# A graph network's edge loop: which edge rows GpSimd gathers, and where the first of them come from

## The chip, the cores and the metric

The kernel runs on one core of one Trainium2 chip. The metric is the device time of one execution in microseconds (us). The core's engines work side by side, each through its own instructions in order: PE (TensorE), DVE (VectorE), ACT (ScalarE), POOL (GpSimd) and SP (SyncE, which here issues DMAs). ACT and POOL issue DMAs as well. All arithmetic is in float32.

## The reference

One message-passing layer of a graph network with a layer norm ahead of it: 12,500 nodes of 64 features, 412,500 edges of 32 features, sorted by receiver (dst). Cut to what matters:

```python
h = jnp.maximum(_layernorm(x, axis=-1), 0.0)
msg_in = concat([h[src], h[dst], edge_attr_32])           # 64 + 64 + 32
messages = act(msg_in @ W1 + b1) @ W2 + b2                # act is swish
att = softmax(act(msg_in @ Wa1 + ba1) @ Wa2 + ba2, axis=0)  # over all edges
aggregated = segment_sum(messages * att, dst)
out = x + act(concat([h, aggregated]) @ Wu1 + bu1) @ Wu2 + bu2
```

W1 and Wa1 split into three parts, for the sender, the receiver and the edge. The sender's part depends on the node alone, so it can be worked out once per node and looked up per edge.

## The kernel before

**Node stage.** x is read in eight chunks. For each, DVE and ACT normalize the rows (sum, deviation, square, root, reciprocal, cut at zero); PE transposes them into hT (features on the partitions, kept on chip for the whole run); PE multiplies hT with the sender's weights, and SP stores the result as the table ts_d, one row of 128 floats per node (L274). Then PE and DVE make the receiver's table, and ACT's queue stores it as tr_d (L310, L312), and behind it one copy of hT as hT_d (L313), which is read only by the function general, a fallback that doesn't run here. Both tables are double buffered tiles of one pool; the main loop's own tiles take that pool's place, so DVE's first preparations (L421 and on) wait for the last tr_d stores.

**Main loop** (one_pass). The 412,500 edges make 3304 tiles of 125 edges, eight to a group, 413 groups (g). load(g) does what can be done ahead, two groups early (AHEAD = 2):
- POOL issues one indirect DMA per tile (L533), which gathers 125 rows of ts_d, by the sender numbers in src_full, into the group's buffer gs. There are seven such buffers, used in turn; a group's first gather waits until the group seven earlier has let go of the buffer. The tile j = 3 gathers 126 rows (WIDE), one more than it uses.
- SP loads the edges' features (eo, L544) and receiver numbers (dbs, L547) for four groups at a time, and for each group two windows of the receivers' table (wins, L554).
- DVE turns receiver numbers into a selection matrix (L558), and PE multiplies it and the edge features with the windows (L562): what the receivers and edges add, in PSUM (pe).

begin(g): DVE adds the gathered rows (L573) and ACT takes tanh (L576). end(g): DVE forms the messages (L586), and the attention logits (L592, L594, L597); L592 is the last to read gs. Four groups later by_node, out_of, project and put weigh the messages and add them into per-node sums. In the first four groups ACT also fills the two tables for these sums, a quarter each time (L752, twice 1588 columns).

**Chosen groups.** In some groups the last tile isn't gathered. Every third group (EVERY, PHASE: g mod 3 = 1, from 8 to NG - 13) is chosen; POOL then issues seven gathers. For the eighth tile, SP loads the 125 sender numbers (num, L478), DVE works out the sender's column in hT and its half (places, L487 to L493), ACT reads the columns' numbers into registers and copies the 125 columns of hT one by one (columns, L504), DVE clears the wrong half (L567), and PE multiplies them with the sender's weights into the same PSUM tile (L568). The copies are spread over earlier groups: burst(g, 0) after begin and burst(g, 1) after end, by the lists in SLOTS.

The order on DVE, ACT and PE is the program's where an instruction is pinned (pin, keep_in_program_order); what isn't pinned, the DMA issues among it, is placed by a scheduler as early as its inputs allow.

Of the kernel before, what the change touches and what calls it, by code (L numbers as in the profile page):

```python
# [44 lines left out]
F32 = mybir.dt.float32  # L45
I32 = mybir.dt.int32
AF = mybir.ActivationFunctionType
ALU = mybir.AluOpType
# [5 lines left out]
P = 128  # L54
# [18 lines left out]

EVERY = 3
PHASE = 1
SLOTS = (((0, 24), (24, 24)), ((48, 24), (72, 12)), ((84, 24), (108, 17)))
ROUND = 12582912.0
WIDE = 126
EPS = 1e-5
# [11 lines left out]
def gnn_kernel(ctx: ExitStack, tc: tile.TileContext, n_edges, x, src, src_row, dst, dst_row, first, edge,  # L91
# [71 lines left out]


    with tc.tile_pool(name="node1", bufs=1) as node1, \
            tc.tile_pool(name="node", bufs=2) as node, \
# [39 lines left out]

        eps = node1.tile([P, 1], F32, name="eps")
        nc.vector.memset(eps, EPS)
# [103 lines left out]
        pin(nc.scalar.dma_start(tr_d[NP:, :], zero[:WR, :]))  # L312
        pin(nc.scalar.dma_start(hT_d, hT))  # L313

# [79 lines left out]
def one_pass(tc, n_edges, v):  # L394
    nc = tc.nc
    NB, T, NG, NP, NT = (v[k] for k in ("NB", "T", "NG", "NP", "NT"))
    ident, iota_w, bj, dloc, src_full, base_sb, real, unreal, far, wrong = (
        v[k] for k in ("ident", "iota_w", "bj", "dloc", "src_full", "base_sb", "real", "unreal",
                       "far", "wrong"))
# [12 lines left out]
    with ExitStack() as ctx:  # L412
# [43 lines left out]
        with tc.tile_pool(name="work2", bufs=2) as work2, \  # L456
# [14 lines left out]

            chosen = {g for g in range(8, NG - 12) if g % EVERY == PHASE}

            def numbers(g):
                if g in chosen:
                    e = (g * K + K - 1) * EP
                    n = nums[g] = small.tile([P, EP], I32, name="num", bufs=2)
                    nc.sync.dma_start(n, bass.AP(tensor=v["src_row"].tensor,  # L478
                                                 offset=v["src_row"][:, e:].offset, ap=[[0, P], [1, EP]]))

            def places(g):
                if g not in chosen:
                    return
                n = nums[g]
                near = small.tile([1, EP], F32, name="near", bufs=1)
                to = small.tile([1, EP], I32, name="to", bufs=2)
                pin(nc.vector.tensor_scalar(to, n[0:1], 1, None, op0=ALU.logical_shift_right))  # L487
                m = NB // 2
                pin(nc.vector.tensor_scalar(near, to, 1.0 / m, 0.5 / m - 0.5, op0=ALU.mult, op1=ALU.add))
                pin(nc.vector.tensor_scalar(near, near, ROUND, None, op0=ALU.add))  # L490
                pin(nc.vector.tensor_scalar(near, near, ROUND, float(1 - m * P), op0=ALU.subtract, op1=ALU.mult))
                pin(nc.vector.scalar_tensor_tensor(to, to, float(P), near, op0=ALU.mult, op1=ALU.add))
                pin(nc.vector.tensor_scalar(n, n, 1, None, op0=ALU.bitwise_and))  # L493
                cols[g] = small.tile([P, EP], F32, name="cols", bufs=2), to

# [10 lines left out]
            def burst(g, k):  # L506
                for i in range(EVERY):
                    columns(g + 3 + i, *SLOTS[EVERY - 1 - i][k])

# [6 lines left out]
            def registers(g, engine, at, base=base_sb, top=NP - 1):  # L516
# [4 lines left out]
                for i in range(n):  # L521
                    at[g + i] = regs[i]

            def load(g):

                t = g * K
                if g % NQ == 0:
                    registers(g, ENG.SP, at_sp)
                full = gather.tile([P, K, C], F32, name="gs")
                gs = gss[g] = full[:EP]  # L530
                for j in range(K - (g in chosen)):
                    rows = WIDE if j == 3 else EP
                    nc.gpsimd.indirect_dma_start(  # L533
                        out=full[:rows, j, :], out_offset=None, in_=ts_d[:, :],
                        in_offset=bass.IndirectOffsetOnAxis(ap=src_full[:rows, t + j:t + j + 1], axis=0))
                if g % NQ == 0:
# [24 lines left out]
                for q in range(H):  # L561
                    pin(nc.tensor.matmul(pe[:, 2 * q:2 * q + 2, :], eo[:, q * EP:(q + 1) * EP],  # L562
                                         win[:, q // 2, :, :], start=True,
                                         stop=q < H - 1 or g not in chosen))
                if g in chosen:
# [4 lines left out]
            def begin(g):  # L570

                n = K - (g in chosen)
                pin(nc.vector.tensor_tensor(gss[g][:, :n, :], pes[g][:, :n, :], gss[g][:, :n, :], ALU.add))  # L573
                if n < K:
                    pin(nc.vector.tensor_copy(gss[g][:, n, :], pes[g][:, n, :]))
                pin(nc.scalar.activation(pes[g], gss[g], AF.Tanh))  # L576
# [161 lines left out]
            for g in range(NG):  # L738
# [39 lines left out]
                for t in {NG - 5: [0, 1], NG - 4: [2, 3], NG - 2: range(4, NT)}.get(g, []):  # L778
                    inputs(t)
                if g == min(30, NG):  # L780
                    pin(nc.vector.tensor_reduce(far[:, 0:1], dloc, AX.X, ALU.max))
                    pin(nc.vector.tensor_scalar(far[:, 0:1], far[:, 0:1], -float(R - 1), None,
                                                op0=ALU.add))
# [357 lines left out]
```

## Time and profile before

| | |
|---|---|
| median of 3 runs (lowest, highest) | 4832.74 us (4832.67, 4833.29) |
| the profiled execution, its own time | 4832.74 us |
| its span in the profile | 4831.0 us |
| busy: POOL, DVE, PE, ACT | 78%, 71%, 50%, 46% |
| gathers on POOL | 3173, mean 1183 ns |
| mean DMA rate | 82 GB/s |

Busy shares are means over the span. In a row of a group of instructions the columns are: line, engine, operation, tiles written and read, shape, count, then busy us and mean ns of one, then the engine's idle time just before these instructions and what ended most of it. "issue" is time in which the engine waited for nothing that the profile shows. In a timeline the columns are start, duration, engine, line, operation, tiles, count and the idle time before in brackets. POOL's time for a gather is the time of issuing it, not that of moving the rows.

### The profile page before, as it was taken

The page shows a single profiled execution, that of the slowest core. Times are in us where ns is not written, and L with a number is a line of the kernel's source. Part 1 is how long each engine was busy: PE and PEld are TensorE (multiplying, and loading weights), DVE is VectorE, ACT ScalarE, POOL GpSimd, SP SyncE. Part 2 cuts the span into 40 slices and gives each one's busy share as a digit, 9 for nine tenths or more (in the row PEclk, how much of TensorE's full clock was granted, in tenths as well). Part 3 has the DMA queues.
Part 4 walks back from the last instruction along what each step waited for, and adds up shares of the span by engine and source line. Part 5 has one row for each costly group of instructions (what it writes and reads, how often), then busy time and mean ns, then how long its engine had stood idle before and what let it go on. Part 6 is the DMA issues. An engine that isn't in the chain of part 4 may idle for free. (4 is left out here: it accounts for less than half of the span.)

```text
span 4831.0 us, 81829 instructions
## 1 busy us (share of the span) xinstructions
PE 2424.5 (50%) x11509; PEld 1945.6 (40%) x11509; DVE 3435.4 (71%) x9793; ACT 2202.4 (46%) x17625; POOL 3770.8 (78%) x3198
## 2 busy tenths in 40 slices
PE   5455555555555444444544554544444444445455
PEld 4344444344444433333433443433333334434344
DVE  6677777777777676766766776776776767767677
ACT  3444444444444444444444444444444444444412
POOL 4777777777777777777777777777777777777775
PEclk8555566666555556665566555566666566555666
DMA  7333333333333333333333333333333333333333
GB/s 253 77 78 85 88 77 85 90 76 84 85 75 78 73 75 78 71 76 78 72 76 77 70 78 78 69 78 78 70 78 73 75 78 71 76 77 72 76 93 82
DMA packets 364009, 395.99 MB, mean 82 GB/s; under 512 B 213813, under 2 KB 293236, under 8 KB 363074
## 3 DMA queue, kind: packets, MB, share of 16 engines
q0 software_dynamic: 240624, 206.55, 19.3%
q1 hardware_dynamic: 121458, 174.49, 15.3%
q10 hardware_dynamic: 1376, 9.67, 0.5%
q14 instruction: 457, 3.74, 0.3%
q8 instruction: 94, 1.54, 0.1%
HBM read 361.63 MB, written 25.72 MB: 80 GB/s over the span
## 5 line engine op out<-in xcount | busy, mean ns | idle before, releaser
L533 POOL DMA_INDIRECT gs<-ts_d,src_sb x3173 | 3753.7, 1183 | 1018.5 <-issue 957.7
L562 PE MATMUL pe<-wins,eo 128*125 128x256 f32 x3304 | 1523.6, 637 | 1522.4 <-DVE eo L558 1256.3
L504 ACT COPY cols<-hT 128x1 f32 x16375 | 1619.4, 187 | 739.3 <-issue 735.7
L562 PEld LDWEIGHTS pe<-wins,eo 128*125 128x125 f32 x3304 | 997.8, 319 | 1843.4 <-DVE eo L558 1342.9
L573 DVE TENSOR_TENSOR gs<-pe,gs 125x1024 f32<-125x1024 f32 (+1 forms) x413 | 487.3, 1180 | 1067.3 <-DMA gs<-ts_d,src_sb 1053.4
L576 ACT ACTIVATE pe<-gs 125x1024 f32<-125x1024 f32 x413 | 424.3, 1027 | 1695.8 <-DVE gs L573 831.0
L640 DVE TENSOR_SCALAR wt<-iota_w,dloc,p 125x40 f32<-125x40 f32 x3304 | 766.3, 352 | 1.8
L646 PE MATMUL sp<-wt,acts 125*65 125x40 f32 x6608 | 648.6, 269 | 13.1 <-DVE wt L640 11.6
L646 PEld LDWEIGHTS sp<-wt,acts 125*65 125x65 f32 x6608 | 608.4, 185 | 23.8 <-DVE wt L640 19.6
L657 PEld LDWEIGHTS mt<-ss,w2u 65*128 65x128 f32 x826 | 209.4, 281 | 349.2 <-issue 206.1
L616 PE MATMUL mt<-ident,mx 125*128 125x125 f32 x110 | 48.1, 438 | 589.5 <-DVE sums L675 563.1
L558 DVE TENSOR_SCALAR eo<-dbs,bj 64x250 f32<-64x250 int32 x826 | 301.0, 395 | 17.7 <-DMA dbs<-in_dst_row_dram 8.3
L657 PE MATMUL mt<-ss,w2u 65*128 65x40 f32 x826 | 187.8, 321 | 250.5 <-DVE gm L623 213.2
L594 DVE TENSOR_TENSOR pe<-pe,w_all 125x512 f32<-125x512 f32 x413 | 288.7, 699 | 13.7
L592 DVE SCALAR_TENSOR_TENSOR pe<-pe,gs 125x512 f32<-125x512 f32 x413 | 287.1, 695 | 10.8
L586 DVE SCALAR_TENSOR_TENSOR acts<-pe,gs 125x512 f32<-125x512 f32 x413 | 283.8, 687 | 12.1 <-ACT pe L576 2.6
L597 DVE TENSOR_REDUCE lg<-pe 125x8 f32<-125x512 f32 x413 | 284.1, 688 | 10.8
L616 PEld LDWEIGHTS mt<-ident,mx 125*128 125x128 f32 x110 | 20.0, 182 | 600.6 <-issue 597.5
L678 DVE COPY stand<-nmax 64x40 f32 x826 | 211.5, 256 | 3.3
L675 DVE TENSOR_TENSOR sums<-sums,mt 64x40 f32 x606 | 114.1, 188 | 4.9 <-PE mt L657 0.8
L671 DVE SCALAR_TENSOR_TENSOR sums<-sums,scale,mt 64x40 f32 x220 | 55.7, 253 | 84.6 <-PE mt L657 82.5
L357 DVE TENSOR_SCALAR bu<-mt,w_all 64x256 f32<-64x256 f32 (+1 forms) x50 | 23.9, 477 | 92.0 <-PE mt L348 91.6
(124 smaller groups left out, 1106.8 us busy)
## 6 DMA issues: line engine op xcount, KB each, us to landing
eo<-in_edge_dram SPq DMA_DIRECT2D x103, 500.0 KB
dbs<-in_dst_row_dram SPq DMA_DIRECT2D x206, 250.0 KB
gs<-ts_d,src_sb POOLq DMA_INDIRECT x3173
wins<-tr_d SPq DMA_DIRECT2D x826, 32.0 KB
num<-in_src_row_dram SPq DMA_DIRECT2D x131, 62.5 KB
ts_d<-ts SPq DMA_DIRECT2D x5, 896.0 KB
tr_d<-tr ACTq DMA_DIRECT2D x5, 896.0 KB
hT_d<-hT ACTq DMA_DIRECT2D x1, 3136.0 KB
```

The lines of the kernel that those rows point to most:

```text
L504: pin(nc.scalar.copy(to[:, first + i:first + i + 1], hT[:, bass.ds(regs[i], 1)]))
L533: nc.gpsimd.indirect_dma_start(out=full[:rows, j, :], out_offset=None, in_=ts_d[:, :], in_offset=bass.IndirectOffsetOnAxis(ap=src_full[:ro ...
L558: pin(nc.vector.tensor_scalar(eo[:WR, e], db[:, e], bj[g // NQ % 2 * WR:(g // NQ % 2 + 1) * WR, g, h:h + 1], None, op0=ALU.is_equal))
L562: pin(nc.tensor.matmul(pe[:, 2 * q:2 * q + 2, :], eo[:, q * EP:(q + 1) * EP], win[:, q // 2, :, :], start=True, stop=q < H - 1 or g not in ...
L573: pin(nc.vector.tensor_tensor(gss[g][:, :n, :], pes[g][:, :n, :], gss[g][:, :n, :], ALU.add))
L576: pin(nc.scalar.activation(pes[g], gss[g], AF.Tanh))
L592: pin(nc.vector.scalar_tensor_tensor(att, th[:, :, 0:U], 1.0, gs[:, :, 0:U], op0=ALU.add, op1=ALU.mult))
L594: pin(nc.vector.tensor_tensor(att, att, wa2[:EP, None, :].to_broadcast([EP, K, U]), ALU.mult))
L597: pin(nc.vector.tensor_reduce(lgs[s][:, k:k + K], att, AX.X, ALU.add))
L640: pin(nc.vector.tensor_scalar(wt[:, j, :], iota_w[:EP, j // H, :], dloc[:, g * K + j:g * K + j + 1], p[:, k + j:k + j + 1], op0=ALU.is_equ ...
L646: pin(nc.tensor.matmul(sp, acts[g % ACTS][:, j, :], wt[:, j, :], start=j == 0, stop=j == K - 1))
L657: pin(nc.tensor.matmul(pp, w2u.rearrange("s h u -> s (h u)"), sps.pop(g), start=True, stop=True))
```

## The change

There are two groups of edits.

- The 126-row gather is dropped: all gathers have 125 rows. The chosen groups are two of every five (g mod 5 = 1 or 4) in place of one of three; their 125 columns are copied in five lots of 24, 24, 24, 24 and 29, two lots in each group, in the five bursts from five groups ahead on. The small tiles num, to and cols have three buffers instead of two.
- Groups 0 to 3 do not use ts_d. Right at the start ACT's queue loads the sender numbers of their 32 tiles, and POOL gathers rows of the input x itself (64 floats). In load(g) the new function features normalizes these rows on the edges, PE transposes them, and PE multiplies them with the sender's weights into pe; begin(g) copies pe instead of adding. The store of hT_d leaves ACT's queue and is written in the loop, in seven pieces at g = 20 to 26, on SP.

```diff
@@ -71,11 +71,11 @@
-EVERY = 3
-PHASE = 1
-SLOTS = (((0, 24), (24, 24)), ((48, 24), (72, 12)), ((84, 24), (108, 17)))
+LOTS = ((0, 24), (24, 24), (48, 24), (72, 24), (96, EP - 96))
+ROUNDS = 5
+SLOTS = {1: ((5, 1), (4, 0), (4, 1), (3, 0), (3, 1)), 4: ((5, 0), (5, 1), (4, 0), (4, 1), (3, 0))}
 ROUND = 12582912.0
-WIDE = 126
+RAW = 4
 EPS = 1e-5
@@ -161,6 +161,15 @@
+
+    raw_src = const.tile([P, RAW * K], I32, name="raw_src")
+    nc.scalar.dma_start(raw_src, src[:, :RAW * K])
+    raws = [gather.tile([P, K, C], F32, name="gs") for _ in range(RAW)]
+    for g in range(RAW):
+        for j in range(K):
+            nc.gpsimd.indirect_dma_start(
+                out=raws[g].rearrange("p k c -> p (k c)")[:EP, j * D:(j + 1) * D], out_offset=None, in_=x[:, :],
+                in_offset=bass.IndirectOffsetOnAxis(ap=raw_src[:EP, g * K + j:g * K + j + 1], axis=0))
@@ -204,7 +213,7 @@
-        eps = node1.tile([P, 1], F32, name="eps")
+        eps = const.tile([P, 1], F32, name="eps")
@@ -310,7 +319,6 @@
         pin(nc.scalar.dma_start(tr_d[NP:, :], zero[:WR, :]))
-        pin(nc.scalar.dma_start(hT_d, hT))
@@ -469,12 +477,12 @@
-            chosen = {g for g in range(8, NG - 12) if g % EVERY == PHASE}
+            chosen = {g for g in range(8, NG - 12) if g % ROUNDS in SLOTS}
                     e = (g * K + K - 1) * EP
-                    n = nums[g] = small.tile([P, EP], I32, name="num", bufs=2)
+                    n = nums[g] = small.tile([P, EP], I32, name="num", bufs=3)
                     nc.sync.dma_start(n, bass.AP(tensor=v["src_row"].tensor,
@@ -483,7 +491,7 @@
                 near = small.tile([1, EP], F32, name="near", bufs=1)
-                to = small.tile([1, EP], I32, name="to", bufs=2)
+                to = small.tile([1, EP], I32, name="to", bufs=3)
                 pin(nc.vector.tensor_scalar(to, n[0:1], 1, None, op0=ALU.logical_shift_right))
@@ -491,7 +499,7 @@
                 pin(nc.vector.tensor_scalar(n, n, 1, None, op0=ALU.bitwise_and))
-                cols[g] = small.tile([P, EP], F32, name="cols", bufs=2), to
+                cols[g] = small.tile([P, EP], F32, name="cols", bufs=3), to
@@ -504,8 +512,10 @@
             def burst(g, k):
-                for i in range(EVERY):
-                    columns(g + 3 + i, *SLOTS[EVERY - 1 - i][k])
+                for i in (3, 4, 5):
+                    slots = SLOTS.get((g + i) % ROUNDS, ())
+                    if (i, k) in slots:
+                        columns(g + i, *LOTS[slots.index((i, k))])
@@ -521,18 +531,43 @@
+            def features(g):
+
+                gs = gss[g] = v["raws"][g][:EP]
+                xg, xm = (gs[:, h * H:(h + 1) * H, :].rearrange("p k (r d) -> p (k r) d", d=D) for h in range(2))
+                total = small.tile([EP, K], F32, name="raw_t", bufs=1)
+                pin(nc.vector.tensor_reduce(total, xg, AX.X, ALU.add))
+                pin(nc.vector.scalar_tensor_tensor(xm, total[:, :, None].to_broadcast([EP, K, D]), -1.0 / D, xg,
+                                                   op0=ALU.mult, op1=ALU.add))
+                pin(nc.scalar.activation(xg, xm, AF.Square))
+                rstd = small.tile([EP, K], F32, name="raw_r", bufs=1)
+                pin(nc.vector.tensor_reduce(rstd, xg, AX.X, ALU.add))
+                pin(nc.scalar.activation(rstd, rstd, AF.Sqrt, bias=v["eps"][:EP], scale=1.0 / D))
+                pin(nc.vector.reciprocal(rstd, rstd))
+                pin(nc.vector.scalar_tensor_tensor(xg, xm, 0.0, rstd[:, :, None].to_broadcast([EP, K, D]),
+                                                   op0=ALU.max, op1=ALU.mult))
+                pt = one_ps.tile([P, 4, P], F32, name="mt")[:, :, :EP]
+                for q in range(H):
+                    pin(nc.tensor.transpose(pt[:, q, :], xg[:, 2 * q:2 * q + 2, :], ident[:EP, :EP]))
+                to = raw_to[g] = v["raws"][g][:, H:, :EP]
+                pin(nc.scalar.copy(to, pt))
+
+            raw_to = {}
+
             def load(g):
                     registers(g, ENG.SP, at_sp)
-                full = gather.tile([P, K, C], F32, name="gs")
-                gs = gss[g] = full[:EP]
-                for j in range(K - (g in chosen)):
-                    rows = WIDE if j == 3 else EP
+                if g < RAW:
+                    features(g)
+                else:
+                    gss[g] = gather.tile([P, K, C], F32, name="gs")[:EP]
+                gs = gss[g]
+                for j in range(0 if g < RAW else K - (g in chosen)):
                     nc.gpsimd.indirect_dma_start(
-                        out=full[:rows, j, :], out_offset=None, in_=ts_d[:, :],
-                        in_offset=bass.IndirectOffsetOnAxis(ap=src_full[:rows, t + j:t + j + 1], axis=0))
+                        out=gs[:, j, :], out_offset=None, in_=ts_d[:, :],
+                        in_offset=bass.IndirectOffsetOnAxis(ap=src_sb[:, t + j:t + j + 1], axis=0))
                 if g % NQ == 0:
@@ -561,7 +596,10 @@
                                          win[:, q // 2, :, :], start=True,
-                                         stop=q < H - 1 or g not in chosen))
+                                         stop=g >= RAW and (q < H - 1 or g not in chosen)))
+                    if g < RAW:
+                        pin(nc.tensor.matmul(pe[:, 2 * q:2 * q + 2, :], raw_to[g][:, q, :], v["w_pair"][:, 0],
+                                             start=False, stop=True))
                 if g in chosen:
@@ -570,7 +608,10 @@
                 n = K - (g in chosen)
-                pin(nc.vector.tensor_tensor(gss[g][:, :n, :], pes[g][:, :n, :], gss[g][:, :n, :], ALU.add))
+                if g < RAW:
+                    pin(nc.vector.tensor_copy(gss[g], pes[g]))
+                else:
+                    pin(nc.vector.tensor_tensor(gss[g][:, :n, :], pes[g][:, :n, :], gss[g][:, :n, :], ALU.add))
                 if n < K:
@@ -777,6 +818,10 @@
                     inputs(t)
+                if 20 <= g < 27:
+                    n = -(-(NB // 2) // 7)
+                    q = slice((g - 20) * n, min((g - 19) * n, NB // 2))
+                    nc.sync.dma_start(v["hT_d"][:, q, :], v["hT"][:, q, :])
                 if g == min(30, NG):
```

The short hunk that passes src_sb in place of src_full to one_pass is left out.

More of the change, by code (lines that the diff above doesn't have):

```diff
@@ L396, in one_pass @@
     NB, T, NG, NP, NT = (v[k] for k in ("NB", "T", "NG", "NP", "NT"))
-    ident, iota_w, bj, dloc, src_full, base_sb, real, unreal, far, wrong = (
-        v[k] for k in ("ident", "iota_w", "bj", "dloc", "src_full", "base_sb", "real", "unreal",
+    ident, iota_w, bj, dloc, src_sb, base_sb, real, unreal, far, wrong = (
+        v[k] for k in ("ident", "iota_w", "bj", "dloc", "src_sb", "base_sb", "real", "unreal",
                        "far", "wrong"))
```

## The prediction

> **What bounds the kernel now.** I read the page first, then the instructions of the gather line, POOL's timeline, and the start of the run in ten-microsecond windows and as a timeline.
>
> ```profile
> span 4831.0 us, 81829 instructions
> ...
> L533 POOL DMA_INDIRECT gs<-ts_d,src_sb x3173 | 3753.7, 1183 | 1018.5 <-issue 957.7
> ...
> L504 ACT COPY cols<-hT 128x1 f32 x16375 | 1619.4, 187 | 739.3 <-issue 735.7
> ...
> L573 DVE TENSOR_TENSOR gs<-pe,gs 125x1024 f32<-125x1024 f32 (+1 forms) x413 | 487.3, 1180 | 1067.3 <-DMA gs<-ts_d,src_sb 1053.4
> ```
>
> POOL does almost nothing but issue gathers. DVE, the busiest of the others, waits for gathered rows (1053 of 1067 us). POOL's own idle time is "issue": no engine holds it. The next two answers are the gather line's first and last start, and POOL's timeline (start, duration, idle before).
>
> ```profile
> L533 POOL DMA_INDIRECT gs<-ts_d,src_sb x3173: 992/1209/1646, 51.0 to 4773.4; - x199
> ```
>
> ```profile
> 1008.37 1.22 POOL L533 DMA_INDIRECT gs<-ts_d,src_sb  x1 [0.30 <-issue]
> 1009.89 0.99 POOL L533 DMA_INDIRECT gs<-ts_d,src_sb  x1 [0.30 <-issue]
> 1011.19 1.21 POOL L533 DMA_INDIRECT gs<-ts_d,src_sb  x1 [0.30 <-issue]
> 1012.70 1.21 POOL L533 DMA_INDIRECT gs<-ts_d,src_sb  x1 [0.30 <-issue]
> ```
>
> One gather in each group is short: 1.30 us from start to start where the others take 1.51. It is the one of 126 rows (j = 3); groups with seven gathers keep it at that place. From 51.0 to 4773.4 there are 3172 intervals: 413 of 1.30 us, 2759 long ones, and 3.0 us of extra waits between 85 and 93 us (rows with 1.66, 1.71 and 0.50 us idle, released by earlier gathers' DMAs). So a long interval is (4722.4 - 3.0 - 413 x 1.30) / 2759 = 1.516 us with its small disturbances. After the last gather's start 57.6 us remain.
>
> The start, by windows (columns: window, length, busy PE, PEld, DVE, ACT, POOL, clock, DMA share, GB/s), then by timeline:
>
> ```profile
> 50.00:60.00 10.00, 9.91 (x46) 8.41 (x46) 6.39 (x12) 0.00 (x0) 7.19 (x6) 1.00 0.74 272
> 60.00:70.00 10.00, 8.63 (x39) 6.76 (x37) 6.32 (x11) 0.00 (x0) 8.13 (x7) 1.00 0.82 291
> 70.00:80.00 10.00, 0.16 (x1) 0.00 (x0) 3.76 (x23) 0.00 (x0) 7.86 (x8) 0.72 0.93 348
> ```
>
> ```profile
> 74.17 0.89 ACTq L313 DMA_DIRECT2D hT_d<-hT  x1
> ...
> 77.11 0.40 DVE L421 MEMSET bases<- 1x414 int32 x1 [4.00 <-DMA tr_d<-tr]
> ...
> 83.71 0.22 DVE L470 COPY w2u<-mt 65x64 f32<-65x64 f32 x1
> 92.20 1.12 DVE L558 TENSOR_SCALAR eo<-dbs,bj 64x250 f32<-64x250 int32 x4 [8.27 <-DMA dbs<-in_dst_row_dram]
> ...
> 97.83 1.23 DVE L573 TENSOR_TENSOR gs<-pe,gs 125x1024 f32<-125x1024 f32 x1 [4.51 <-PE pe L562]
> ...
> 102.21 0.70 DVE L592 SCALAR_TENSOR_TENSOR pe<-pe,gs 125x512 f32<-125x512 f32 x1
> ```
>
> The main loop's compute cannot begin before the tr_d stores have landed (77.1); DVE then prepares its tiles until 83.9 and waits for dbs, which lands behind the hT_d store. Group 0's buffer is last read by L592, until 102.9. That costs nothing now: seven buffers hold 56 gathers, so POOL needs it back only at about 137.
>
> **Count and pace of the gathers.** Chosen groups rise from 131 to 157 (g mod 5 = 1: 78, = 4: 79, between 8 and 400), so the main stream loses 26 gathers, and 32 more leave it for the early ones: 3173 - 58 = 3115. All now have 125 rows. The first saves 58 x 1.516 = 87.9 us, the second costs 413 x (1.516 - 1.30) = 89.2 us. The two cancel: 3115 x 1.516 = 4722 us, against 4722 + 1 now. So the time hangs on when the main stream runs without a stop.
>
> **The early gathers.** Their row indices are 16 KB; the first x chunk (256 KB) is issued at 0.92 and used at 3.74, so I put their arrival at 3.7. No row shows a gather of 256-byte rows; I take the 125-row interval: 3.7 + 32 x 1.514 = 52 us, as ts_d is ready (51.0). Bounds: 1.30 us each (done at 45, then waiting for ts_d) and 2.4 (done at 80). Either is free as long as POOL must stop later anyway, which is the next point. The Trainium skill (DMA: Bandwidth & Descriptors, Specifications) puts the least transfer for line rate at 512 B; half rows speak against this edit, but no run here shows it and it moves none of the terms.
>
> **The new wait.** The early gathers fill four of the seven buffers. Groups 4, 5 and 6 take the other three: 52 + 24 x 1.514 = 88.5. Group 7 then needs group 0's buffer, and POOL is in order: every later gather queues behind that one. Its release, in the new order on DVE, from 83.9 with durations of the same shapes (reduction or combination of 125x512: 0.69; a square of 512: 0.63; a square root of 8: 0.30; reciprocal 0.19; four transposes 1.12; copy 0.59; L558 twice 0.8; eight matmuls 3.75):
> - features(0): reduce, centre, square, reduce, root, reciprocal, scale = 4.2, to 88.1; transposes and copy to 89.9; L558 beside them, to 89.0.
> - features(1) to 93.1 on DVE; PE's group 0 matmuls to 94.2; group 0's copy (1.2, from L573) to 95.4.
> - ACT: copy of features(1) to 95.9, table load 1.28, tanh 1.03 to 98.2, then the two table fills of L752 (1.51 each) to 101.2. All stand in order ahead of features(2)'s square, 101.8.
> - features(2), which load(2) puts ahead of end(0): reduce 102.6, second table load to 103.1, root, reciprocal, scale to 104.4; L558 to 105.2; L586 and L592 to 106.7.
>
> So POOL's group 7 starts at 106.7 where it could have at 88.5. Group 8 needs end(1), by the same steps at 118.6; POOL gets there 12.1 us after group 7, at 118.8: no second stop. From group 2 on no features stand in the way.
>
> The ACT table load of before takes 1.28 us and tanh follows at once (99.12, then 100.42), after idle time. The Trainium skill (ScalarE: Activation LUTs, What ACT_TABLE_LOAD costs) adds a drain of 1.38 us to every switch; by that, two exposed switches would make the release 2.8 us later and the total 2.8 us more. I go by the row.
>
> **What moves that chain.** The seven pieces of the hT_d store are not pinned. In the built order they stand on SP right behind the last ts_d store and ahead of the first edge load, not at groups 20 to 26; so they are issued from about 48 us, beside the tr_d stores on ACT's queue (49 to 74). They no longer stand in front of dbs, which is then there before DVE asks. But tr_d ends the wait at 77.1. The store's 3136 KB at the 432 GB/s of the window 10 to 20 us is 7.4 us of all DMA engines; the windows above leave free 2.6 + 1.8 + 0.5 = 4.9 us. Bounds for the delay of tr_d: nothing (it fits the gaps), 2.5 (gaps full) and 7.4 (tr_d stands behind all of it). I take 4.5, between the last two, because DVE already waits for these stores five times (1.74, 1.15, 2.37, 0.71, 2.19 us). The early gathers meet the x loads while the DMA share is 0.79 to 1.04; DVE waits 0.44 us for the third chunk: I add 0.7 (0 to 2).
>
> Release: 106.7 + 4.5 + 0.7 = 112.
>
> **What I cost at nothing.** 26 more chosen groups: on ACT 26 x (1619 + 739) / 131 = 468 us, or 1.1 us a group on top of (2202 + 736) / 413 = 7.1, of 11.5; on DVE six place operations, one mask and one copy, 2.1 us each time, 0.13 us a group on 8.3. POOL's pace covers both; without that cover they would be 468 and 55 us. On SP, 26 more num loads (about 0.4 us of issue each) and the seven hT_d issues (under 0.9 us each, in the stretch from 47.7 to 77 where SP issues nothing). The end of the run (57.6 us) has no chosen group and stays.
>
> **Sum.** From group 7's first gather 3115 - 24 = 3091 are left, 3090 intervals: last start 112 + 3090 x 1.516 = 4796.4, now 4773.4: +23 us. Span 4854; the profiled execution took 4832.74, its span plus 1.7, which is also the median of the three runs: **4855.7 us**. In general the change is the release minus 89.0 us.
>
> **Rivals.**
> 1. Not slower: group 0's buffer comes free early, because the features run ahead of the tr_d stores' end or tanh isn't held. It decides below 98.7 us (+9.7 us, 0.2%, about what a measurement can tell from no change); floor 88.5. Time 4832 to 4842. For: dbs is early now. Against: DVE's order has the features behind the tiles of 83.9, and fourteen steps follow. 0.08.
> 2. The hT_d store fits the gaps: release 107.4, 4851 us. For: the DMA share there is 0.74 to 0.82. 0.25.
> 3. Compute no longer keeps up in groups with 53 columns: 1% over POOL's pace in all groups would be 47 us: 4903. Against: 8.3 of 11.5 us on the fullest engine. 0.05.
> 4. The fourth gather is short for its place, not its rows. Then 413 x 0.216 = 89 us come back: 4767. Against: nothing else sets it apart. 0.03.
> 5. The start is worse still (release beyond 120, as when early gathers hold the x loads): above 4864. 0.04.
> The forecast itself has 0.55.
>
> **Range.** Release 102 (no delay, and steps 5 us shorter than their rows) to 120 gives +13 to +31; the pace is uncertain by 0.001 us x 3090 = 3 us: 4843 to 4867. Slower by over 0.2%: 0.55 + 0.25 + 0.05 + 0.04 = 0.89; within: 0.08; faster: 0.03.
>
> **What would show it.** No gather of 1.00 us in the main stream and a steady 1.51; 32 gathers from about 4 to 52 us; an idle stretch of POOL of some 20 us before the 25th main gather, released by DVE near 112; hT_d issued about 48 us; tr_d's last wait later than 77.1. If POOL runs on through 90 us, or waits for buffers in mid-run, I am wrong.

## The result, and the profile after

The changed kernel takes **4863.53 us** (median of four runs, 4860.96 to 4864.56), the kernel before 4832.97 beside it (four runs, 4832.67 to 4833.29): ratio 1.0062, 95% interval [1.0045, 1.008]. It is slower by more than 0.2%, as forecast; the time lies inside the range and 7.8 us above the number. The profiled execution took 4863.94 us, its span 4862.2 against 4831.0: +31.2 where +23 was forecast.

The page of the changed kernel first (gathers are now L568, column copies L512, the addition of gathered rows L614):

```profile
span 4862.2 us, 88819 instructions
...
L568 POOL DMA_INDIRECT gs<-ts_d,src_sb x3115 | 3775.1, 1212 | 972.1 <-issue 893.4
...
L512 ACT COPY cols<-hT 128x1 f32 x19625 | 1925.2, 187 | 959.4 <-issue 936.9
...
L614 DVE TENSOR_TENSOR gs<-pe,gs 125x1024 f32<-125x1024 f32 (+1 forms) x409 | 478.9, 1171 | 1012.5 <-DMA gs<-ts_d,src_sb 1001.0
```

Fewer gathers with a longer mean take about as long as before (3775 us, 3754 before), and DVE still waits 1001 us for gathered rows. So POOL is still the bound, and 26 more chosen groups cost ACT and DVE nothing that counts. POOL's idle time is no longer all "issue"; its waits, by releaser (sum in us, times, longest in us):

```profile
POOL gs L568 <- issue: 893.4, 2930, 0.3
POOL gs L568 <- DVE pe L635: 23.8, 5, 22.6
```

One wait of 22.6 us is the new thing. POOL's timeline shows its place, and what comes ahead of it and after:

```profile
45.15 4.91 POOL L170 DMA_INDIRECT gs<-in_x_dram,raw_src  x1 [0.30 <-issue]
...
58.04 1.21 POOL L170 DMA_INDIRECT gs<-in_x_dram,raw_src  x1 [0.30 <-issue]
59.55 1.21 POOL L568 DMA_INDIRECT gs<-ts_d,src_sb  x1 [0.30 <-issue]
...
94.53 1.28 POOL L568 DMA_INDIRECT gs<-ts_d,src_sb  x1 [0.30 <-issue]
118.42 1.21 POOL L568 DMA_INDIRECT gs<-ts_d,src_sb  x1 [22.61 <-DVE pe L635]
...
129.01 1.21 POOL L568 DMA_INDIRECT gs<-ts_d,src_sb  x1 [0.30 <-DVE pe L633]
```

The early gathers end at 59.2 instead of 52. Groups 4 to 6 follow at once; then POOL stands still until 118.42, where 112 was forecast. Group 8 (129.01) waits no second time. The gather line's answer (min/median/max ns, first and last start) has no 126-row gather left and gives the pace:

```profile
L568 POOL DMA_INDIRECT gs<-ts_d,src_sb x3115: 1205/1209/1684, 59.5 to 4805.2; - x195
```

From 118.42 to 4805.2 there are 3090 intervals of 1.5168 us (forecast 1.516); 57.0 us follow the last start (57.6). Last, the timeline of the start, all engines, for the chain that ends in the release (by the program, L633 is the last to read group 0's buffer; it ends at 117.47, 0.95 us ahead of POOL's gather, and the view names L635, the next instruction of DVE, which ran meanwhile):

```profile
45.06 3.59 DVE L203 TENSOR_TENSOR dloc<-dst_sb,base_p 125x3304 f32<-125x3304 int32 x1
51.63 2.47 DVE L317 TENSOR_TENSOR tr<-pn,w_all 128x512 f32<-128x512 f32 x4
52.21 8.13 SPq L824 DMA_DIRECT2D hT_d<-hT  x7
...
88.38 0.40 DVE L429 MEMSET bases<- 1x414 int32 x1 [4.44 <-issue]
94.99 0.69 DVE L539 TENSOR_REDUCE raw_t<-gs 125x8 f32<-125x512 f32 x1
106.27 1.22 DVE L612 COPY gs<-pe 125x1024 f32<-125x1024 f32 x1 [2.17 <-PE pe L601]
109.60 1.51 ACT L793 ACTIVATE sums<-start 128x1588 f32<-128x1588 f32 x1
111.02 1.51 ACT L793 ACTIVATE stand<-start 128x1588 f32<-128x1588 f32 x1
113.06 1.28 ACT L545 ACT_TABLE_LOAD   x1
114.36 0.30 ACT L545 ACTIVATE raw_r<-raw_r,eps 125x8 f32<-125x8 f32 x1
116.77 0.70 DVE L633 SCALAR_TENSOR_TENSOR pe<-pe,gs 125x512 f32<-125x512 f32 x1
```

The receivers' numbers (L203) start at 45.06; the same instruction of before starts at 40.95. The first tr operation comes at 51.63 (before 47.64). From there to the first preparation after the tr_d stores (88.38), which I call the tr stretch, it is 36.75 us, before 29.47 (47.64 to 77.11). All seven pieces of the hT_d store are issued at 52 to 60 us, between these two, and none at groups 20 to 26. From the first reduction of the features (94.99) to the end of L633 (117.47) the chain takes 22.5 us, as it was worked out.

### The profile page after: what moved, and what is told of

The parts are those of the page before. It is cut to its first block, busy times and chain, and to the rows that moved or that the text cites. A ratio compares the mean times of both kernels' runs of the same rounds, so it can differ in the third digit from the quotient of the medians.

```text
span 4862.2 us, 88819 instructions
## 1 busy us (share of the span) xinstructions
PE 2447.0 (50%) x11609; PEld 1966.1 (40%) x11609; DVE 3519.7 (72%) x10021; ACT 2514.4 (52%) x20891; POOL 3838.3 (79%) x3172
## 5 line engine op out<-in xcount | busy, mean ns | idle before, releaser
L568 POOL DMA_INDIRECT gs<-ts_d,src_sb x3115 | 3775.1, 1212 | 972.1 <-issue 893.4
L512 ACT COPY cols<-hT 128x1 f32 x19625 | 1925.2, 187 | 959.4 <-issue 936.9
L614 DVE TENSOR_TENSOR gs<-pe,gs 125x1024 f32<-125x1024 f32 (+1 forms) x409 | 478.9, 1171 | 1012.5 <-DMA gs<-ts_d,src_sb 1001.0
L681 DVE TENSOR_SCALAR wt<-iota_w,dloc,p 125x40 f32<-125x40 f32 x3304 | 779.2, 368 | 1.2
L687 PE MATMUL sp<-wt,acts 125*65 125x40 f32 x6608 | 653.2, 270 | 12.3 <-DVE wt L681 10.3
L635 DVE TENSOR_TENSOR pe<-pe,w_all 125x512 f32<-125x512 f32 x413 | 288.7, 699 | 13.8
L633 DVE SCALAR_TENSOR_TENSOR pe<-pe,gs 125x512 f32<-125x512 f32 x413 | 287.2, 695 | 10.7
L627 DVE SCALAR_TENSOR_TENSOR acts<-pe,gs 125x512 f32<-125x512 f32 x413 | 283.8, 687 | 10.7 <-ACT pe L617 1.4
L606 PEld LDWEIGHTS pe<-stack,cols 128*125 128x125 f32 x314 | 92.7, 295 | 25.6
```

The source lines that it names most:

```text
L512: pin(nc.scalar.copy(to[:, first + i:first + i + 1], hT[:, bass.ds(regs[i], 1)]))
L568: nc.gpsimd.indirect_dma_start(out=gs[:, j, :], out_offset=None, in_=ts_d[:, :], in_offset=bass.IndirectOffsetOnAxis(ap=src_sb[:, t + j:t ...
L633: pin(nc.vector.scalar_tensor_tensor(att, th[:, :, 0:U], 1.0, gs[:, :, 0:U], op0=ALU.add, op1=ALU.mult))
L635: pin(nc.vector.tensor_tensor(att, att, wa2[:EP, None, :].to_broadcast([EP, K, U]), ALU.mult))
L681: pin(nc.vector.tensor_scalar(wt[:, j, :], iota_w[:EP, j // H, :], dloc[:, g * K + j:g * K + j + 1], p[:, k + j:k + j + 1], op0=ALU.is_equ ...
L687: pin(nc.tensor.matmul(sp, acts[g % ACTS][:, j, :], wt[:, j, :], start=j == 0, stop=j == K - 1))
```

## The experiments

Twelve kernels ran in three sets, each set on another chip, and a ratio is always against the kernel before on the same chip. On the first chip it took 4833.93 us, within 1 us of the time beside the result, so there I also compare with the 4863.53 us of the changed kernel. On the second it took 4860.54 (4841.69 to 4865.88, 17 runs), on the third 5230.97 (5175 to 5240); there I compare parts of the traces, and say so. Edits are shown against the changed kernel, and for the three named "before" against that one. No kernel leaves work out; rows beyond 125 land in partitions that nobody reads.

**The short gather alone.** Is the fourth gather short for its 126 rows, and does the change's loss of these rows carry its price?

```
-        gss[g] = gather.tile([P, K, C], F32, name="gs")[:EP]
+        full = gather.tile([P, K, C], F32, name="gs")
+        gss[g] = full[:EP]
...
+        rows = 126 if j == 3 else EP
-            out=gs[:, j, :], out_offset=None, in_=ts_d[:, :],
-            in_offset=bass.IndirectOffsetOnAxis(ap=src_sb[:, t + j:t + j + 1], axis=0))
+            out=full[:rows, j, :], out_offset=None, in_=ts_d[:, :],
+            in_offset=bass.IndirectOffsetOnAxis(ap=v["src_full"][:rows, t + j:t + j + 1], axis=0))
```

> The changed kernel with one thing put back: the tile j = 3 of groups 4 to 412 gathers 126 rows again. My theory (a gather's time on POOL goes by its rows: 1.30 us from start to start with 126, 1.516 with 125, and POOL sets the pace): 409 gathers x 0.216 us = 88 us less than the changed kernel's 4863.5, so 4775 us; the stop of POOL ahead of group 7 stays, about 1 us longer since POOL gets there earlier. Rival (the fourth gather was short for its place, or compute with two chosen groups of five can't follow a faster POOL): 4863, or between 4775 and 4863 with DVE no longer waiting for gathers.

Measured: 4775.63 us (4775.15 to 4776.72), ratio 0.988 [0.9865, 0.9895]. Its page:

```profile
span 4773.4 us, 88819 instructions
L570 POOL DMA_INDIRECT gs<-ts_d,src_sb x3115 | 3685.5, 1183 | 972.9 <-issue 896.6
```

The mean gather is 1183 ns again, as in the kernel before, and 88 us are gone with the wait at the start still there (23.59 us). So the change with the 126th row put back is faster than both kernels. Rival 4 falls: with 125 rows in the fourth place the gather was long, with 126 it is short.

**The early gathers alone.** Without them (RAW = 0, and no raw gathers ahead of the node stage) POOL should meet no wait, and the node stage should be on time again.

```
-RAW = 4
+RAW = 0
...
-    raws = [gather.tile([P, K, C], F32, name="gs") for _ in range(RAW)]
+    raws = []
```

> The changed kernel without the early gathers: groups 0 to 3 gather ts_d rows like the rest, features and the extra matmuls are gone; chosen groups and 125 rows as in the changed kernel, hT_d pieces still right behind ts_d. My theory: the node stage goes back to its old times (first gather at 51 to 52 us, first tr_d piece on DVE at 47.6 instead of 51.6), POOL makes no stop, and 3146 intervals x 1.516 us = 4769 follow: last start 4821, span 4878, time about 4880. So the early gathers would be worth 16 us in the changed kernel, not the 48.5 us that 32 intervals are. Rival (the early gathers only cost: they delay the node stage and make POOL stop, and give nothing): at or below 4863. Rival on the node stage (it is late for the hT_d store and not for the early gathers): first gather near 55 us here too.

Measured: 4880.72 us (4879.86 to 4882.81), ratio 1.0098 [1.0083, 1.0114]. The first gather starts at 49.94 and no stop follows. The receivers' numbers start at 41.15 and the first tr operation at 47.72, the times of before: the lateness of the node stage (4.0 us) belongs to the early gathers. The tr stretch is 34.9 us (to 82.58), still above the 29.5 of before: most of the 7.3 us is not theirs. And the early gathers gain: 32 x 1.516 = 48.5 us taken from the main stream, less 9.6 (first main gather 59.55, not 49.94), less 22.4 (the stop), leaves 16.5 us; the two times differ by 17.2.

**The hT_d store really late.** Pinned, its pieces stay at groups 20 to 26.

```
-                    nc.sync.dma_start(v["hT_d"][:, q, :], v["hT"][:, q, :])
+                    pin(nc.sync.dma_start(v["hT_d"][:, q, :], v["hT"][:, q, :]))
```

> The changed kernel with the hT_d store's seven pieces pinned on SP, so that they stand at groups 20 to 26. My theory (beside the tr_d stores they take DMA time from them): the stretch from the first tr_d piece on DVE to the first preparation (36.8 us in the changed kernel, 29.5 in the kernel before) goes back to about 30, group 0's buffer comes free about 7 us earlier (111 instead of 118.4), and the time falls by as much, to 4856.5; the pieces at groups 20 to 26 cost nothing, since POOL doesn't wait there. Rival (the tr_d stores are slow for the early gathers' backlog, or the store fits the gaps): the stretch stays near 36 us and the time at 4863.

Measured: 4854.07 us, ratio 1.0041 [1.0028, 1.0055]: 9.5 us less than the changed kernel. The tr stretch is 28.1 us (51.14 to 79.23), and POOL goes on at 108.86 instead of 118.42, 9.56 earlier:

```profile
108.86 1.21 POOL L568 DMA_INDIRECT gs<-ts_d,src_sb  x1 [13.11 <-DVE pe L635]
```

So the store issued at 52 us costs 8.6 us of the tr stretch, and about 9.5 of the time, all through the release. The pieces, now issued between 249 and 313 us, show no cost there: the time falls by as much as the release moves. The 4.5 us that the forecast gave this store were too little. Not all of it is waiting for stores: late in the stretch DVE waits for PE, whose granted clock there is low (two rows of the changed kernel):

```profile
75.32 1.29 DVE L317 TENSOR_TENSOR tr<-pn,w_all 128x512 f32<-128x512 f32 x2 [2.33 <-PE pn L315]
70.00:80.00 10.00, 8.48 (x25) 6.96 (x26) 5.69 (x10) 0.00 (x0) 8.04 (x7) 0.66 0.86 293
```

From 70 to 80 us the clock (third figure from the right) is 0.66. With the store pinned, PE has done most of these products by 70 us, at a clock of 1.00 in the window from 60 to 70.

**One buffer more.** An eighth gather buffer (and seven of another pool's eight, for the room) moves the wait from group 7 to group 8.

```
-    gather = ctx.enter_context(tc.tile_pool(name="gather", bufs=7))
+    gather = ctx.enter_context(tc.tile_pool(name="gather", bufs=8))
...
-    ACTS, WINS, AHEAD = 8, 3, 2
+    ACTS, WINS, AHEAD = 7, 3, 2
```

> The changed kernel with eight gather buffers instead of seven (and seven acts buffers instead of eight, to make room). My theory (POOL stops because groups 4 to 6 use up the buffers before group 0's comes free at 118.4): POOL now goes on through group 7, stops eight gathers later, at about 108 instead of 95.9, and goes on at 118.4 as before, one group further: 8 x 1.516 = 12.1 us less, 4851.4 us. Rival (the stop costs nothing, because compute is behind anyway and would make POOL wait later): 4863.

Measured: 4851.27 us, ratio 1.0036 [1.0022, 1.005], 12.3 us less than the changed kernel. POOL's timeline:

```profile
106.95 1.21 POOL L568 DMA_INDIRECT gs<-ts_d,src_sb  x1 [0.30 <-issue]
118.43 1.21 POOL L568 DMA_INDIRECT gs<-ts_d,src_sb  x1 [10.27 <-DVE pe L635]
```

The release is where it was, 118.4. POOL only gets to the wait later, one group of eight gathers (12.1 us) further on. This is the mechanism of the forecast, a buffer held by the chain, seen from the other side.

**The rows in the kernel before.** All gathers with 125 rows:

```
-                    rows = WIDE if j == 3 else EP
+                    rows = EP
```

> The kernel before with one edit: the tile j = 3 gathers 125 rows like the others. My theory (the pace on POOL goes by rows, nothing else is near its limit): 413 x (1.516 - 1.301) = 89 us more than 4833, so 4922 us, with all gathers near 1.209 us. Rival (the fourth place is what makes it short, or the 126th row is only a side effect of something else in the change): 4833.

Measured on the second chip: 4930.8 us, ratio 1.0158 [1.0131, 1.0186]. By the medians it is 70 us more than the kernel before on that chip, whose runs spread over 24 us; 89 were expected. In the trace the first and last gather start 4819.9 us apart, 4722.3 in the trace of before from the first chip: 97.6, of which 413 x 0.216 = 89 are the rows, and most of the rest a slightly longer interval on that chip. The dropped row has a price in either kernel; its size in the kernel before is less certain than the 88 us of the first experiment.

**Rows by place**, one run: 125, 126, 127 and 128 rows, by j mod 4.

```
-                    rows = WIDE if j == 3 else EP
+                    rows = EP + j % 4
```

> The kernel before with 125, 126, 127 and 128 rows in turn over the tiles j = 0 to 3 and again 4 to 7; the extra rows land in partitions that nothing reads. It is to show what sets a gather's issue time. If it goes by how evenly the rows divide over the DMA engines (the Trainium skill, DMA: Bandwidth & Descriptors, Why a DMA increments its semaphore by 16 and not by 1: the largest number up to 16 that divides the row count, so 5, 14, 1 and 16), then 125: 1.21 us, 126: 1.00, 127 longest, 128 shortest or like 126. If only odd against even counts: 127 like 125, 128 like 126. If any count above 125 is short: all three others near 1.00. Time by the second: 3173 gathers, half at 1.516 and half at 1.30 from start to start: about 4833 - 0.215 x (1540 - 413) = 4590 us; in the first case anywhere, for the 127 rows.

POOL's timeline, the first four gathers of one group:

```profile
1001.59 1.21 POOL L533 DMA_INDIRECT gs<-ts_d,src_sb  x1 [0.30 <-issue]
1003.11 0.99 POOL L533 DMA_INDIRECT gs<-ts_d,src_sb  x1 [0.30 <-issue]
1004.41 2.56 POOL L533 DMA_INDIRECT gs<-ts_d,src_sb  x1 [0.30 <-issue]
1007.27 0.96 POOL L533 DMA_INDIRECT gs<-ts_d,src_sb  x1 [0.30 <-issue]
```

In this order they have 125, 126, 127 and 128 rows: 1.21, 0.99, 2.56 and 0.96 us. 127 rows take over twice as long as 126, so it is not the amount. Count and place go together in this run, but the place alone is ruled out by the runs around it: with 125 rows everywhere no place is short, and with 126 everywhere (next) all are near 1.00. The run took 5698.28 us.

**All gathers with 126 rows.** If POOL's issue were the only bound, this would be some 600 us faster.

```
-                    rows = WIDE if j == 3 else EP
+                    rows = WIDE
```

> The kernel before with 126 rows in every tile; the 126th row is read by nothing. My theory (POOL's pace is the only limit): 2759 x 0.215 = 593 us less, 4240 us, at 1.30 us a gather and 10.0 us a group, which compute (DVE 8.3 us a group) still follows. Rival (another limit comes up between 11.4 and 10.0 us a group: the time a gather's rows need to land, or DVE with its waits): the time ends between 4240 and 4833, POOL's idle time grows, and DVE's waits for gathers (1067 us before) go to nothing if it is DVE.

A miss on the whole line: 5921.24 us, ratio 1.2198 [1.2165, 1.2232]. The gathers did become short, but POOL waits for buffers (its semaphore wait ahead of a group's gathers has a median of 7.4 us, 0.04 in the kernel before), and ACT is slow by itself. The groups of that kernel's trace:

```profile
L533 POOL DMA_INDIRECT gs<-ts_d,src_sb x3173 | 3174.0, 1000 | 2644.2 <-issue 2505.8 <-DMA ts_d<-ts 48.4 <-ACT cols L504 20.4
L504 ACT COPY cols<-hT 128x1 f32 x16375 | 1906.7, 188 | 3016.2 <-issue 3001.6 <-PE pe L562 4.0 <-DVE pe L592 3.0
L573 DVE TENSOR_TENSOR gs<-pe,gs 125x1024 f32<-125x1024 f32 (+1 forms) x413 | 486.2, 1177 | 61.3 <-issue 29.6 <-remote 20.0 <-DMA gs<-ts_d,src_sb 1.6
```

DVE no longer waits for gathers (1.6 us). The column copies, which run one after another in the kernel before, come singly here, with 0.5 to 1.2 us of idle time ahead of each that the trace puts down to no other engine ("issue", 3001.6 us in all, 735.7 before; 757.1 on this same chip with 125 rows everywhere). ACT's timeline:

```profile
2000.73 0.19 ACT L504 COPY cols<-hT 128x1 f32 x1 [0.54 <-issue]
2001.44 0.19 ACT L504 COPY cols<-hT 128x1 f32 x1 [0.52 <-issue]
2002.18 0.19 ACT L504 COPY cols<-hT 128x1 f32 x1 [0.55 <-issue]
2003.56 0.19 ACT L504 COPY cols<-hT 128x1 f32 x1 [1.19 <-issue]
```

The trace does show where the delay sits. Ahead of each copy ACT works out its address in registers (FUSED_REGOPS; min/median/max ns); here are the kernel before on the first chip, this kernel, and the changed kernel as it ran on the third chip (below):

```profile
L504 ACTq FUSED_REGOPS  x16375: 37/37/43, 126.2 to 4608.4; - x200
L504 ACTq FUSED_REGOPS  x16375: 3/37/1402, 168.3 to 5713.3; - x200
L512 ACTq FUSED_REGOPS  x19625: 2/37/934, 141.0 to 4843.6; - x199
```

The median stays at 37 ns, but where 43 was the most, single ones now take up to 1402, and one in eight takes over 300 (12.7%; on this same chip with 125 rows everywhere 0.3%). So POOL's pace covers an ACT that can become the bound. Why ACT's register operations slow down beside such gathers stays open.

**The table fills moved** from groups 0 to 3, where they stand in the release chain, to groups 4 to 7.

```
-                if g < 4:
+                if 4 <= g < 8:
```

> The changed kernel with ACT's fills of the two per-node tables moved from the groups 0 to 3 to the groups 4 to 7 (the first sums are put in at group 7, after its fill). My theory (the two fills of group 0 stand ahead of the square of features(2) on ACT, and end(0) behind features(2) on DVE): group 0's buffer comes free 2.9 us earlier, POOL's stop is as much shorter, 4860.6 us; group 8's wait for end(1) can't grow, since it also loses its fills. Rival (the release is held by something else than that chain): stop of 22.6 us and 4863.5 us unchanged.

Measured on the second chip: 4867.61 us, ratio 1.0025 [1.0012, 1.0038]. The time can't tell 2.9 us there: its interval was 1.5187 us instead of 1.5168, 5.9 us over 3090 intervals. The trace can. From group 0's copy (L612, 103.43) to POOL's next gather (112.75) it is 9.32 us, in the changed kernel 12.15 (106.27 to 118.42): 2.83 us less. The two fills are in the chain at nearly their full length.

**All together.** The hT_d store pinned, eight buffers, the fills later, and 126 rows in one place (j = 3), then in two (`rows = 126 if j in (1, 5) else EP`).

> The changed kernel with what shortens POOL's stop put together (hT_d pieces pinned at groups 20 to 26, eight gather buffers with seven acts buffers, ACT's table fills at groups 4 to 7) and 126 rows in the tile j = 3. My theory: group 0's buffer comes free at about 106 (108.8 with the late hT_d store, less 2.8 for the fills), and POOL needs it at 59.1 + 32 x 1.49 = 106.7: no stop is left. Against the kernel with 126 rows and a stop of 23.3 us (4775.6) that is 4752 us where the kernel before takes 4833, a ratio of 0.983. Rival (a later buffer, or compute in the first groups, stops POOL again): a stop shows elsewhere before 200 us, and the time is above 4760.

> The same with 126 rows in two tiles of a group, j = 1 and j = 5. If POOL's pace is still the only limit: 409 x 0.214 = 88 us less than the kernel with one such tile, about 4664 us, ratio 0.965, 11.1 us a group. Rival (with all tiles at 126 rows ACT's column copies came 0.5 to 1.2 us apart instead of 0.1 and the time was 5921; what slows them grows with the share of 126-row gathers): ACT's idle time before the copies (959 us in the changed kernel for 19625 copies) grows by several hundred us, and POOL waits for buffers or not according to whether ACT stays below 11 us a group.

Both missed, on the third chip: 5251.25 us, ratio 1.0073 [0.9995, 1.0151], and 5488.86, ratio 1.0532 [1.046, 1.0604]. The part that the edits were for came out in the first: from 50 to 221 us POOL's gathers start less than 2 us apart. From 221 us on POOL waits for buffers (a median of 6.6 us ahead of a group's gathers). The page of that kernel:

```profile
L570 POOL DMA_INDIRECT gs<-ts_d,src_sb x3115 | 3696.3, 1187 | 1374.8 <-issue 1326.9
...
L512 ACT COPY cols<-hT 128x1 f32 x19625 | 2191.2, 188 | 2023.2 <-issue 1923.7
```

ACT's gaps are back (1923.7 us of issue; 936.9 in the changed kernel on the first chip). With two places of 126 rows they are 2144.7. Whether that is the kernel or the chip, the last run tells.

**The changed kernel again**, unaltered, on the third chip, and with it one edit: early gathers of 128 rows, in case their uneven spread delays the node stage.

```
-                out=raws[g].rearrange("p k c -> p (k c)")[:EP, j * D:(j + 1) * D], out_offset=None, in_=x[:, :],
-                in_offset=bass.IndirectOffsetOnAxis(ap=raw_src[:EP, g * K + j:g * K + j + 1], axis=0))
+                out=raws[g].rearrange("p k c -> p (k c)")[:, j * D:(j + 1) * D], out_offset=None, in_=x[:, :],
+                in_offset=bass.IndirectOffsetOnAxis(ap=raw_src[:, g * K + j:g * K + j + 1], axis=0))
```

> The changed kernel unaltered, beside the other three on the same chip: 1.0062 of the kernel before; it is the base for the three above, since the run with the later fills was on a chip on which a gather took 1.212 instead of 1.209 us. Theory and rivals expect the same of it.

> The changed kernel with 128 rows in the early gathers (the last three land in partitions that nothing reads); the 3115 gathers of the main stream keep 125. It is about the node stage, which is 4 us late when the early gathers run (DVE reaches the receiver numbers at 45.1 instead of 41.0). If that comes from how 125 rows spread over the DMA engines: back to 41 to 42 us, the early gathers done near 45 us at 1.26 us each, release of group 0's buffer 3 to 4 us earlier, 4860 us. If it comes from the many 256-byte rows as such: 45 us or later again, and 4863.

The unaltered kernel took 5050.05 us there, ratio 0.9686 [0.9622, 0.9751]. That is a miss, and of the other sign: on this chip the change is 3.1% faster, where 1.0062 was expected. Its page:

```profile
L568 POOL DMA_INDIRECT gs<-ts_d,src_sb x3115 | 3775.5, 1212 | 1134.4 <-issue 1060.7
...
L512 ACT COPY cols<-hT 128x1 f32 x19625 | 2167.3, 187 | 1879.2 <-issue 1777.6
...
L614 DVE TENSOR_TENSOR gs<-pe,gs 125x1024 f32<-125x1024 f32 (+1 forms) x409 | 478.0, 1169 | 36.7 <-DMA gs<-ts_d,src_sb 13.3
```

The same program has 1777.6 us of issue gaps at its copies where it had 936.9, and DVE's wait for gathers is gone (13.3 us, on the first chip 1001). The start is nearly the same (the stop from 93.3 to 118.7). DVE waits 356 us for the column copies here (L605 and L627), 0.4 on the first chip, and POOL waits for buffers again. So on this chip ACT's copies have become the bound; by its time that holds for the kernel before as well, but no trace of it from there exists, and why the change gains there isn't shown. What the combined version takes where POOL is the bound wasn't measured; the first experiment's 4775.63 us is the best measured time beside that chip's 4833.93.

The 128 early rows took 5211.75 us (ratio 1.0 [0.9934, 1.0066]). Each early gather is shorter (mean 1092 ns, beside 1398 in the unaltered kernel there), but the receivers' numbers start at 52.51, not 45.43, and POOL goes on at 125.24 after 25.79 us idle. So it gives no earlier node stage; ACT and DVE have waits in that stretch whose releaser the trace doesn't name, so this run doesn't settle what in the early gathers delays the node stage. It settles something else: it differs from the unaltered kernel in 32 gathers of the first 60 us, and takes 162 us longer, of which the later release is 6.5. The rest lies in the main loop, where the two programs are the same (ACT's issue time at the copies 1886.8 us, 1777.6 unaltered). So on the third chip a difference of some 160 us can't be put down to an edit, and the times of the two combined versions there stay unexplained.

## Why the prediction was right, and which sizes were off

- **The bound: right.** POOL's pace sets the time; the compute of 26 more chosen groups is covered (DVE waits 1001 us for gathers). On another chip the cover is gone, and with it the sign of the change, which no row of the first chip's trace showed; the prediction is right for the chip of its profile.
- **Count against pace: right.** 3115 gathers of 125 rows cost what 3173 with 413 short ones cost. The 88 us on each side were found apart: adding the row back gives 4775.63. The interval was 1.5168, not 1.516: 2.4 us over 3090.
- **The early gathers: mechanism right, size short.** They took 3.79 to 59.2 us, not 3.7 to 52 (mean 1.44 us each, one of 4.91). As said, this cost POOL nothing, since it had to stop later anyway. What was off is the sentence "I add 0.7 (0 to 2)" for the node stage: measured 4.0, twice the upper bound. The cause is theirs (without them it is gone). I had looked only at DVE's wait for the third x chunk. The trace now has ACT waiting 3.00 us for a ts_d store by 28.66, where the first such wait of before is 0.62 us, at 37.97; that this is the whole path of the delay is not shown.
- **The new wait: right** in its group (7), place (before the 25th main gather), releaser and single occurrence. The chain by durations, 22.8 us from the end of preparations, came out at 22.5, with another 0.95 until POOL's gather started. The two table fills were rightly in it (2.83 of 3.0 us came back when they were moved).
- **The hT_d store: mechanism right, size short.** It is issued at 52 us and delays tr_d. "I take 4.5, between the last two" measured 7.3 beside before, and 8.6 beside the same kernel with the store pinned late. The 7.3 is near the bound of 7.4 by chance: DVE's waits for tr_d in the stretch sum to 17.0 us (with the 4.44 ahead of L429) where they were 12.2, so 4.8 more, about what was taken; its waits for PE sum to 3.8 where they were 1.3, and this 2.5 had no term in the sum. That the low clock alone makes it is not shown.
- **The sum.** Release 118.4 instead of 112: 3.3 us from the node stage, 2.8 from the tr stretch, the remaining 0.3 from the chain and the wake-up less the preparations. Then 2.4 from the pace, less 0.6 at the end: 8.2, the whole difference of the spans (4862.2 against 4854).
- **Rivals.** The release did not come below 98.7 (rival 1), the store did not fit the gaps (2), compute did not fall behind on that chip (3), the short gather is not for its place (4). Rival 5 (release beyond 120, x loads held up) names part of what happened, short of its limit.

The rule on table loads (the Trainium skill, ScalarE: Activation LUTs, What ACT_TABLE_LOAD costs) puts a drain of 1.38 us beside each load. The trace disagrees: in the chain above the load starts at 113.06 and the activation behind it at 114.36, 1.30 us later, right behind an earlier ACT instruction. The measurement decides; with two drains, by the page's figure, the chain would have been an estimated 2.8 us longer than it was.

## What to carry to other kernels

Before moving work in front of a stage, ask whose buffers it fills: filling four of seven early only brings the wait forward, and the gain is what is left when the first buffer's whole chain of readers has run. A store or load that isn't pinned goes where the scheduler puts it, so look for its place in the built order before believing a loop index in the source. And test the small shape details by themselves, because here one row more in one gather out of eight was worth as much as 58 gathers. Then ask which engine sets the pace where the kernel will run: on the chip where ACT's copies did, these rules about POOL no longer gave the time.

## What the runs showed of the hardware

**Rows and gather issue.** Gathers of 512-byte rows keep POOL for 1.21, 1.00, 2.56 and 0.96 us at 125, 126, 127 and 128 rows, then 0.30 us until the next. The Trainium skill (DMA: Bandwidth & Descriptors, Why a DMA increments its semaphore by 16 and not by 1) spreads one DMA over the largest number of engines, up to 16, that divides the slowest dimension: 5, 14, 1 and 16 engines for these four. The times fall in exactly that order; the page gives no issue time, so it is a guess, not shown here, that this spread is the cause.

**Early gathers and the loads.** The windows of the changed kernel (columns: window, length, busy PE, PEld, DVE, ACT, POOL, clock, DMA share, GB/s):

```profile
10.00:20.00 10.00, 6.85 (x21) 5.06 (x21) 9.86 (x13) 3.91 (x7) 8.15 (x7) 1.00 1.04 351
20.00:30.00 10.00, 8.23 (x42) 6.52 (x42) 8.73 (x11) 6.08 (x14) 7.89 (x7) 1.00 1.01 329
```

The same windows of the kernel without early gathers:

```profile
10.00:20.00 10.00, 7.08 (x22) 5.24 (x23) 9.53 (x13) 4.50 (x9) 0.00 (x0) 1.00 1.04 431
20.00:30.00 10.00, 9.36 (x49) 7.83 (x49) 9.26 (x12) 7.98 (x18) 0.00 (x0) 1.00 0.57 202
```

With seven gathers of 256-byte rows in 10 us beside the loads, the engines are as busy (1.04) and move 351 GB/s instead of 431; the loads go on to about 30 us. With early gathers of 128 rows, on the third chip, the first window moves 401 (350 unaltered there). So most of the loss goes with the count of rows, not with their 256 bytes.

**ACT's issue gaps.** Register-addressed copies of 0.19 us run one after another on the first chip, and with 0.5 to 1.2 us between single ones when all gathers have 126 rows; on the third chip every kernel traced has such gaps, after one to eleven copies. The trace names no other engine; the register operation ahead of a copy, 43 ns at most in the two kernels on the first chip, takes up to 1.40 us in the kernels with such gaps. It stays open what slows it; it goes with 190 us in the changed kernel (5050 on the third chip, 4863 in the first measurement) and 1060 us in the kernel with all gathers at 126 rows, more than anything this change does.
